# Moving the second half of y behind the third chunk, and the four output products one chunk later, in a Mamba block on one core

## The chip, the cores and the metric

The kernel runs on one core of one Trainium2 chip. The metric is device time in microseconds (us) of one execution, as the median of several runs; less is better. The core has a matrix engine (PE, TensorE; its weight loads are listed apart as PEld), three engines for elementwise work (DVE, VectorE; ACT, ScalarE; POOL, GpSimd), and SP (SyncE), which here only issues transfers. Each engine works through its own queue in order; semaphores tie them together. Matmul results go to PSUM, which has eight banks of 128 x 512 f32.

## The reference, cut to what matters

```python
x = x + attn(cond(x, cond_128, ...), ...)        # the part that this change touches
x = x + ffn(cond2(x, cond_128, ...), ...)

def attn(hidden_states, in_proj_w, conv_weight, ..., norm_weight, out_proj_w):
    proj = einsum('bld,pd->blp', hidden_states, in_proj_w)     # gate z, x, B, C, dt
    xBC = silu(conv(proj[x, B, C]))                            # 4 taps along L
    ...
    def step(state, inp):                                      # 64 heads, 32 steps
        state = state * dA_t + dtx_t * B_t
        return state, einsum('bhpn,bhn->bhp', state, C_t)
    y = ys + x * D
    yn = y * rsqrt(mean(y * y, over a group of 512) + EPS) * norm_weight * silu(gate)
    return einsum('bli,di->bld', yn, out_proj_w)
```

There are 64 sequences of 32 steps with 512 features, 8 groups g of 8 heads each, and 4096 inner features (512 to a group). All data are f32.

## The kernel before

**Tiles and loops.** The 64 sequences are cut into NT = 4 token blocks T of 16 sequences (512 tokens). The main loop (line 939) runs over NI = 32 iterations i, with T, g = divmod(i, 8): one iteration computes one group of heads for one token block. The scan over time is done in closed form: per group, a Gram matrix of B and C, weighted by decays, is multiplied by x. To keep f32 accuracy, the large products run as three f32r products of high and low parts (`mm_split`, line 196: hi by hi, lo by hi, hi by lo). One large product is therefore 12 matmuls of 128 x 512.

**An iteration.** `chunk(i, c)` for c = 0 to 9 (line 429) is one such product of the input projection each: B, C, x0, z0, x1, z1, x2, z2, x3, z3. `evict` (line 460) brings it out of PSUM: a z chunk by one ACT instruction; the B, C and x chunks by one on ACT, three convolution taps on DVE (line 475) and a silu on ACT (line 483). `flip(i, k)` (line 485) transposes x chunk k on DVE into the tile `xs`. `gram(i)` (line 546) makes the Gram matrix in `g_ps` (32 small matmuls), `scan(i)` (line 523) the decays in the tile `src`, on POOL and DVE; `gram_rows` and `decay` (lines 564 and 576) multiply the two.

**y.** `y_part(i, 0, 8)` and `y_part(i, 8, 16)` (line 592) are the two halves of the product of `xs` and `src`: 128 small matmuls of 32 x 32 each (with 128 weight loads), into four banks. The loop over f in it means that the first four matmuls need the x chunks 0 and 1 and the next four the chunks 2 and 3. The first half of iteration i stands at the end of that iteration, the second half in iteration i+1, where it is called with j = i - 1. Then `yend(j, c)`, c = 0 to 3 (line 609), gates a bank of y with z and splits it into `yhi` and `ylo` (a square and a cast on ACT, two instructions on DVE, an addition on POOL); `sumsq(j)` (line 631) reduces the squares.

**Output products.** `out_step(j, bg)`, bg = 0 to 3 (line 909), multiplies `yhi`, `ylo` by the output weights `wo` (`outp`, one large product of 12 matmuls, tile `o`) and adds the result to `acc` on DVE (`outp_end`, line 706, the instruction of line 711). `out_step(j, 1)` first makes the norm's factor: `sumsq2` (line 640), one small matmul `s_ps`, four DVE instructions and a power on POOL. With g = 7 `outp_end` also issues the stores of `acc`, on POOL's queue (on SP's in the last token block).

**Weights of the output product.** `wo_pieces(i)` (line 658) loads `wo` for iteration i in four pieces on SP's queue, one call of `next` a piece. In token block 0 the raw weights are loaded and split by ACT and POOL (`wo_split`, line 679); after that the split weights come from DRAM.

**Order and buffers.** `tc.manual_schedule` (line 922) keeps PE and SP in the order in which the program is written. The other engines' queues are put in order by a planner, from the order of the program and its own estimate of when an instruction can run. Tiles of one tag share a fixed number of buffers: PSUM's tag "mm" has 7 banks, which the chunks, the four banks of a y, the output products and a few others take in turn, the one that was freed first being taken first; `xs`, `src`, `yhi`, `ylo` and `wo` have one buffer each.

PE's order in an iteration from the third on (j > 0) is: chunks 0 and 1, the second half of y(j), chunks 2 and 3, `g_ps`, chunks 4 and 5, o0, chunk 6, `s_ps`, o1, chunk 7, the product of `gram_rows` (`gr_ps`), o2, chunk 8, o3, chunk 9, the first half of y(i). `cond` and `dt_stage` of the next token block, with their own small products, are spread over the iterations with g = 6 and 7, `attend` stands in the one with g = 5.

## Time and profile before

| what | value |
|---|---|
| median of three runs | 1539.41 us (1536.66 to 1543.33) |
| the profiled execution | 1537.98 us, of which the span of all instructions is 1536.2 us |
| PE busy | 98% of the span, mean granted clock 0.993 |
| DVE, ACT, POOL busy | 77%, 41%, 32% |
| DMA engines, mean | 203 GB/s; the instruction queue of PE (q8) 125 packets, 2.05 MB |
| large products of the projection (`mm`, 3840 matmuls) | 926.1 us busy on PE |
| output products (`o`, 1536 matmuls) | 416.0 us busy on PE |
| y (8192 matmuls) | 97.5 us busy on PE |

PE's busy time overstates its work, since matmuls are pipelined: a matmul of 128 x 512 is shown with 390 ns, while two of them start 227 ns apart. A gap of PE is therefore best found in the times at which its loads and matmuls start. The views of waits name for every engine what ended its idle time; "issue" is idle time for which the profile shows no other engine's work as the reason.

### The profile page before, as it was taken

What the parts mean: (1) busy time and instruction counts of PE and PEld (TensorE: products, weight loads), DVE (VectorE), ACT (ScalarE), POOL (GpSimd) and SP (SyncE); (2) the same over time, 40 slices, a digit from 0 to 9 for tenths busy, and PEclk for the clock granted to TensorE, in tenths of its full rate; (3) what the DMA queues carried; (4) which work ended last, traced back from release to release, by engine and by line L of the source; (5) the groups of instructions that cost most, each with busy time, mean ns of one, the idle gap of its engine ahead of it and who ended that gap; (6) DMA issues with size and microseconds to landing.
All of it is one profiled execution on the core that took longest, in us unless ns stands there. A gap on an engine that the chain in (4) does not pass through costs nothing.

```text
span 1536.2 us, 37576 instructions
## 1 busy us (share of the span) xinstructions
PE 1500.2 (98%) x15857; PEld 1226.6 (80%) x15857; DVE 1175.7 (77%) x1869; ACT 637.3 (41%) x1140; POOL 485.4 (32%) x421
## 2 busy tenths in 40 slices
PE   7899999999999999999999999999999999999997
PEld 6788888787788888888878888888888888877776
DVE  7877877888877777779767777887877777777668
ACT  5645555653433333424433332444433323333330
POOL 4656557651522212112331211223242112223105
PEclk9999999999999999999999999999999999999999
DMA  5777777885765555644765555555575555565345
GB/s 205 257 265 272 276 254 260 271 263 186 260 215 198 186 194 193 204 133 150 246 208 191 189 180 179 186 166 178 200 253 186 183 177 166 178 213 173 108 131 172
DMA packets 123305, 311.31 MB, mean 203 GB/s; under 512 B 30528, under 2 KB 42048, under 8 KB 121088
## 3 DMA queue, kind: packets, MB, share of 16 engines
q1 hardware_dynamic: 120320, 301.56, 58.1%
q0 software_dynamic: 2816, 7.34, 1.4%
q8 instruction: 125, 2.05, 0.5%
q14 instruction: 44, 0.36, 0.1%
HBM read 237.02 MB, written 71.83 MB: 201 GB/s over the span
## 4 chain that ended last, share of the span: by engine, by line
PE 86%; DVE 8%; issue 3%; ACT 1%; POOL 1%; DMA 1%; SPq 0%; POOLq 0%; ACTq 0%; DVEq 0%
PE mm L201 53%; PE o L201 21%; PE y L601 6%; DVE x L475 1%; PE fo L201 1%; PE gr_ps L567 1%; DVE ylo L629 1%; PE g_ps L554 1%; PE cv L828 1%; PE h_ps L220 1%; PE d_ps L314 1%; DVE x1s L1211 1%; DVE dt L336 1%; PE lo L871 1%; DVE acc L711 0%
## 5 line engine op out<-in xcount | busy, mean ns | idle before, releaser
L201 PE MATMUL mm<-hid,wsp 128*128 128x512 f32 x3840 | 926.1, 394 | 1.4 <-issue 1.4
L201 PEld LDWEIGHTS mm<-hid,wsp 128*128 128x128 f32 x3840 | 715.5, 189 | 151.3 <-issue 2.1
L625 POOL TENSOR_TENSOR y<-y,y 128x512 f32<-128x512 f32 x96 | 144.4, 1505 | 558.7 <-ACT y L615 554.0
L475 DVE SCALAR_TENSOR_TENSOR x<-mm,xcol,x 128x496 f32<-128x496 f32 (+2 forms) x384 | 271.5, 707 | 36.7 <-ACT x L471 32.3
L201 PE MATMUL o<-wo,yhi 128*128 128x512 f32 x1024 | 278.4, 393 | 0.9 <-ACT wo L682 0.5
L201 PEld LDWEIGHTS o<-wo,yhi 128*128 128x128 f32 x1024 | 189.5, 188 | 40.2 <-ACT wo L682 1.3
L483 ACT ACTIVATE x<-x 128x512 f32<-128x512 f32 x128 | 81.0, 633 | 330.6 <-DVE x L475 329.2
L475 DVE SCALAR_TENSOR_TENSOR B<-mm,pack,B 128x496 f32<-128x496 f32 (+2 forms) x96 | 68.8, 717 | 166.8 <-ACT B L471 164.6
L471 ACT ACTIVATE x<-mm,xcol 128x512 f32<-128x512 f32 x128 | 99.9, 780 | 112.7 <-PE mm L201 111.9
L629 DVE TENSOR_TENSOR ylo<-z,yhi 128x512 fp32r<-128x512 f32 x128 | 142.5, 1114 | 0.5 <-ACT yhi L628 0.4
L201 PE MATMUL o<-wo,ylo 128*128 128x512 f32 x512 | 137.6, 390 | 0.2
L711 DVE SCALAR_TENSOR_TENSOR acc<-o,r,acc 128x512 f32<-128x512 f32 x128 | 95.2, 744 | 32.0 <-POOL r L653 31.9
L601 PEld LDWEIGHTS y<-src,xs 32*64 32x64 f32 x8192 | 89.6, 130 | 33.8 <-issue 26.6
L201 PEld LDWEIGHTS o<-wo,ylo 128*128 128x128 f32 x512 | 96.1, 188 | 21.3 <-DVE ylo L629 1.0
L617 DVE SCALAR_TENSOR_TENSOR z<-y,pack,z 128x512 f32<-128x512 f32 x128 | 94.8, 742 | 20.3 <-ACT y L615 20.2
L653 POOL TENSOR_TENSOR r<-var,mhalf 128x4 f32<-128x4 f32 x32 | 33.8, 1057 | 237.8 <-DVE var L649 237.8
L490 DVE STREAM_TRANSPOSE xs<-x 128x512 f32<-128x512 f32 x128 | 89.8, 702 | 24.4 <-ACT x L483 22.2
L601 PE MATMUL y<-src,xs 32*64 32x32 f32 x8192 | 97.5, 225 | 11.1 <-issue 6.3
L628 ACT CAST yhi<-z 128x512 fp32r<-128x512 f32 x128 | 79.1, 618 | 53.2 <-DVE z L617 53.1
L464 ACT ACTIVATE z<-mm 128x512 f32<-128x512 f32 x128 | 75.8, 593 | 54.7 <-PE mm L201 53.4
L422 POOL TENSOR_TENSOR wsp<-w,wsp 128x512 fp32r<-128x512 f32 x56 | 76.4, 1374 | 57.0 <-ACT wsp L421 56.4
L475 DVE SCALAR_TENSOR_TENSOR C<-mm,pack,C 128x496 f32<-128x496 f32 (+2 forms) x96 | 68.8, 717 | 16.5 <-ACT C L471 14.3
(208 smaller groups left out, 1338.8 us busy)
## 6 DMA issues: line engine op xcount, KB each, us to landing
wsp<-wsp SPq DMA_DIRECT2D x320, 512.0 KB, 4.2
wo<-wos SPq DMA_DIRECT2D x96, 512.0 KB, 4.7
wos<-wo SPq DMA_DIRECT2D x16, 1024.0 KB, 6.2
da<-da SPq DMA_DIRECT2D x124, 128.0 KB, 2.7
w<-in_win_dram SPq DMA_DIRECT2D x48, 256.0 KB, 5.3
wor<-in_wout_dram SPq DMA_DIRECT2D x32, 256.0 KB, 5.1
xr<-in_win_dram SPq DMA_DIRECT2D x24, 256.0 KB, 5.2
acc<-in_x_in_dram SPq DMA_DIRECT2D x4, 1024.0 KB, 6.2
```

The source lines that it names most:

```text
L201: nc.tensor.matmul(o, lhsT=a(k), rhs=b(k), start=j == 0, stop=j == last)
L422: sub_of[n] = nc.gpsimd.tensor_tensor(lo, w, hi.bitcast(F32), ALU.subtract).ins
L471: nc.scalar.activation(t, o, AF.Identity, bias=bias, scale=taps[:, 3:4])
L475: nc.vector.scalar_tensor_tensor(tv[:, :, d:], ov[:, :, : L - d], taps[:, 3 - d : 4 - d], tv[:, :, d:], ALU.mult, ALU.add,)
L483: nc.scalar.activation(t, t, AF.Silu)
L490: nc.vector.transpose(st["xs"][:, :, k], t.rearrange("p (n t) -> p n t", t=L))
L601: nc.tensor.matmul(st["y"][q][64 * f : 64 * f + 64, 32 * n : 32 * n + 32], lhsT=st["xs"][r, n, 2 * f : 2 * f + 2].rearrange("p e x -> p (e ...
L617: nc.vector.scalar_tensor_tensor(z, y, nw_s[:, cc : cc + 1], z, ALU.mult, ALU.mult)
L625: st["add"] = nc.gpsimd.tensor_tensor(y2, st["y2"], y2, ALU.add).ins
L628: nc.scalar.copy(hi, z)
L629: st["lo"] = nc.vector.tensor_tensor(lo, z, hi.bitcast(F32), ALU.subtract).ins
L711: nc.vector.scalar_tensor_tensor(acc[:, bg, :], o, st["r"][:, bg : bg + 1], acc[:, bg, :], ALU.mult, ALU.add)
```

## The change

Two things in the loop are moved; no instruction is added or removed.

The second half of y(j) and the `yend` calls behind it stand after chunk 2 instead of chunk 1 (for j > 0; for j = 0 they stood there before), with `yend` 2 and 3 after chunk 3 and `sumsq` after chunk 4, each one chunk later. The four output products stand after chunks 6, 7, 8 and 9 instead of 5, 6, 7 and 8, so that o3 comes right ahead of the first half of y(i). The start of `wo_pieces(i)`, which needs the buffer that o3 reads, goes from behind chunk 8 to behind chunk 9.

```diff
@@ inner(c)
+            if c == 9:
+                wo_steps = wo_pieces(i)
+                for _ in range(1 if i + 1 < NI else 4):
+                    next(wo_steps)
             if c in (1, 2, 3, 4):
...
-            if c == 8:
-                wo_steps = wo_pieces(i)
-                for _ in range(1 if i + 1 < NI else 4):
-                    next(wo_steps)
@@ the loop
-        if j > 0:
+        chunk(i, 2)
+        inner(2)
+        if j >= 0:
             y_part(j, 8, 16)
             yend(j, 0)
             yend(j, 1)
-        chunk(i, 2)
-        inner(2)
-        if j == 0:
-            y_part(j, 8, 16)
-            yend(j, 0)
-            yend(j, 1)
-        if j > 0:
-            yend(j, 2)
-            yend(j, 3)
...
         chunk(i, 3)
         inner(3)
-        if j == 0:
+        if j >= 0:
             yend(j, 2)
             yend(j, 3)
+        chunk(i, 4)
         if j >= 0:
             sumsq(j)
-        chunk(i, 4)
         inner(4)
...
         chunk(i, 5)
         inner(5)
-        if j >= 0:
-            out_step(j, 0)
...
         if j >= 0:
-            out_step(j, 1)
+            out_step(j, 0)
         next(dt_steps, None)
         chunk(i, 7)
         inner(7)
         if j >= 0:
-            out_step(j, 2)
+            out_step(j, 1)
         step_more()
         chunk(i, 8)
         flip(i, 2)
         if j >= 0:
-            out_step(j, 3)
+            out_step(j, 2)
         inner(8)
...
         chunk(i, 9)
+        if j >= 0:
+            out_step(j, 3)
         inner(9)
         flip(i, 3)
```

PE's order in an iteration is then: chunks 0, 1 and 2, the second half of y(j), chunk 3, `g_ps`, chunks 4, 5 and 6, o0, chunk 7, `gr_ps`, `s_ps`, o1, chunk 8, o2, chunk 9, o3, the first half of y(i).

## The prediction, made before the changed kernel was run

> **What bounds the kernel now.** I read the shares of the engines first, then PE's waits, then the order of time around each of them.

> ```profile
> PE 1500.2 (98%) x15857; PEld 1226.6 (80%) x15857; DVE 1175.7 (77%) x1869; ACT 637.3 (41%) x1140; POOL 485.4 (32%) x421
> ...
> q8 instruction: 125, 2.05, 0.5%
> ```

> ```profile
> PE y L601 <- issue: 6.3, 3, 3.0
> PE y L601 <- DVE xs L490: 4.6, 3, 2.6
> ```

> PE bounds nearly everything, and only its order changes: no matmul is saved, and neighbours of each kind meet as often as before. So the change can only remove or add gaps of PE. I took the start of every load and matmul and, for each product, how much longer it lasted than the median of its kind (2.72 to 2.85 us for 12 large matmuls, 1.42 for half a y). In the stretch that the change reaches, the excess is some 16 us, of three sorts.

> First, the last x chunk turned too late (weight loads at the first halves of y in iterations 5 and 7):

> ```profile
> 279.45 0.21 PEld L601 LDWEIGHTS y<-src,xs 32*64 32x64 f32 x8 [0.35 <-DVE x L475]
> 281.64 1.31 PEld L601 LDWEIGHTS y<-src,xs 32*64 32x64 f32 x120 [1.99 <-DVE xs L490]
> ...
> 374.78 0.21 PEld L601 LDWEIGHTS y<-src,xs 32*64 32x64 f32 x8 [0.35 <-DVE dt L336]
> 377.68 1.31 PEld L601 LDWEIGHTS y<-src,xs 32*64 32x64 f32 x120 [2.69 <-DVE xs L490]
> ```

> Eight loads go, then the ninth waits for `xs`. The excess is 2.12 and 2.83 us, and 0.43 in iteration 1.

> Second, a stop of PE that no engine explains, and what the granted clock does behind it (the windows are the half y and the chunk after it: busy, matmuls, clock, DMA):

> ```profile
> 780.11 1.33 PEld L601 LDWEIGHTS y<-src,xs 32*64 32x64 f32 x123 [0.35 <-issue]
> 784.51 0.20 PEld L601 LDWEIGHTS y<-src,xs 32*64 32x64 f32 x5 [3.07 <-issue]
> ```

> ```profile
> 780.12:784.75 4.63, 1.68 (x130) 1.00 0.92 349
> 784.75:789.19 4.44, 4.44 (x16) 0.62 0.05 17
> ```

> The half y lasts 4.63 instead of 1.42 us, and the next chunk 4.44 instead of 2.81, since the clock fell to 0.62. PE has 32,079 rows in the trace (loads, matmuls, sequencer's own) for the 125 packets of its instruction queue, 257 to a packet of 16,384 bytes. Numbered in order, six stops without a releaser stand before rows 962, 1218, 16321, 22977, 28609 and 30658: all 193 or 194 over a multiple of 256. At each, the row ran 1.27 to 1.48 us after the end of an instruction packet. So PE waited for its next 256 instructions. This falls at y because half a y is 256 instructions in 1.42 us, where a large product is 24 in 2.72.

> Third, o0 had to wait 0.36 us in iteration 7 (`ylo`) and 1.15 in iteration 8 (`wo`, split late on ACT).

> **The change, term by term.** The sum is made for the profiled execution of 1537.98 us (1536.2 span, 1.8 around it), which lies 1.4 below the median; the difference is then taken from the median, 1539.41.

> *Flips.* Between chunk 8 and the first half of y there will be o2, chunk 9 and o3, 8.2 us, instead of o3 and chunk 9, 5.5. That gives nothing by itself where DVE is full. In iterations 5 and 7 it is: from the first `z` to the flip it idled 0.33 and about 1.6 us in 34 and 37. Its queue there:

> ```profile
> 277.25 0.74 DVE L711 SCALAR_TENSOR_TENSOR acc<-o,r,acc 128x512 f32<-128x512 f32 x1
> 277.91 2.21 DVE L475 SCALAR_TENSOR_TENSOR x<-mm,xcol,x 128x496 f32<-128x496 f32 x3
> 280.04 0.74 DVE L711 SCALAR_TENSOR_TENSOR acc<-o,r,acc 128x512 f32<-128x512 f32 x1
> 280.88 0.71 DVE L490 STREAM_TRANSPOSE xs<-x 128x512 f32<-128x512 f32 x1
> ```

> Two things lighten it. The second `acc` is o3's; o3 will end only when y begins, so it falls behind the flip: 0.73. And the three taps of chunk 2 (2.1 us) run while DVE now waits for the second half of y; by the time they end, the old order had 1.25 us of `yend` work done: 0.85 gained. With the 0.1 and some 0.65 of idling, the flips come 1.7 and 2.2 us earlier, so 0.3 and 0.6 of the waits of 2.1 and 2.8 remain. The clock lapse behind the second (the chunk at 379.04 took 4.45, 1.63 too long) goes too, and the 0.43: 0.43 + 1.8 + 2.2 + 1.63 = 6.1 gained. Bounds: 2.1 (only the 0.43 and the clock) to 7.0.

> *o0.* It starts 2.7 us later against `yhi`, `ylo` and the `wo` splits. The splits keep their places in the program; the last `ylo` of an ordinary iteration ended 18.1 us after chunk 0 began, o0 began at 18.7 and will begin at 21.3. Gained 1.5; bounds 0.5 to 1.5.

> *Old instruction stops.* Second halves now begin 24 rows later against the blocks of 256. The stops at 780 (3.2 + 1.63), 1092 (0.39) and 1352 (0.95) lose their alignment: gained 6.2. Those in iteration 1 (its second half isn't moved) and after the loop stay.

> *New instruction stops.* From the rows I placed every boundary. (a) Five iterations (7, 13, 20, 27, 30) get one 11 to 17 rows before the second half, so that the next falls at its end. Before, four lay so (5 to 18 rows ahead): 0, 0, 0.39 and 3.2 us. The 3.2 followed a block that had itself only just landed; the longer way from y to y, 8.4 instead of 5.7 us, prevents that. I take 0.3 each, 1.5; bounds 0 and 4.5. (b) Behind the second half there is now only one chunk ahead of `g_ps`, another 64 rows in 0.39 us:

> ```profile
> 955.64 1.49 PE L601 MATMUL y<-src,xs 32*64 32x32 f32 x128
> 957.05 5.73 PE L201 MATMUL mm<-hid,wsp 128*128 128x512 f32 x24
> 962.72 0.46 PE L554 MATMUL g_ps<-C,B 128*32 128x32 f32 x32
> ```

> Before, a block that began inside the second half had 6.8 us to its end; with one chunk out it has 6.8 - 2.65 = 4.15. Eleven iterations have their boundary 31 to 87 rows into that half. In the same eleven, the packet's start (1.2 to 3.0 us after the block was entered), its length (0.9 to 1.7) and 1.38 us to use gave 3.5 to 5.3 us. Above 4.15 that is 1.14, 0.17, 0.78, 0.48, 0.74, 0.89, 0.19, 0.50, 0.79 and twice nothing: 5.7 lost. Bounds: 0, if the fetch begins earlier, and 11, if DMA is as busy as at the slower half of all fetches.

> [...]

> *At nothing.* PSUM: y's four banks are held one chunk longer, so chunk 3 takes chunk 0's bank; the last tap of B ended 6.1 us after chunk 0's start (638.79 to 644.88), it is needed at 9.8. o3's bank goes to chunk 2, 7 us later; o3's `acc` takes 0.74. If such a cover fails, each microsecond late is one in every iteration. `scan`: `src` is free 2.7 us later, but POOL built it only 7.7 us after y's end (645.87 to 653.61), behind `yend`'s additions, which follow DVE's pace as before. `s_ps`, the norm's factor: shifted with its user. SP: in token blocks 1 to 3 the load of `wo` waits for o3, now 41 us into an iteration, and holds up the load of the next chunk 5, wanted 17 us later (landing 4.2); in block 0 it waits for a raw buffer only. POOL's 20 stores per token block come one chunk later; their readers stand an iteration or more on.

> Sum: -6.1 - 1.5 - 6.2 + 1.5 + 5.7 = -6.6. The profiled execution would take 1531.4, the median 1532.8.

> **Rivals.** (R1) The instruction blocks come in time: 6.6 + 1.5 + 5.7 = 13.8 off, 1525.6. For it: two of eleven were early enough already. Against: the other nine weren't. (R2) DVE stays what the first half of y waits for: where it is full, moving PE's order moves nothing. Then the flips give 0.4 instead of 6.1: 1538.5. For it: 0.33 us of idling in iteration 5. Against: o3's `acc` leaves the queue ahead of the flip. (R3, slower) The planner puts o3's `acc` ahead of the flip, which it precedes in the program, as it did before (280.04 against 280.88). DVE then stands until o3 is done, and y's ninth load waits for 0.44 (o3's end to `acc` at 680.38) + 0.74 + 0.71 less the 0.3 that eight loads and the change of kind take: 1.6 us, in 31 iterations 50: 1583. It decides wherever the planner thinks o3 done when x3's silu is. Against: x3's silu ends some 4 us before o3 does. From five such iterations on, the gain is gone. (R4) The change does less than it says: boundaries drift by a few rows an iteration and new stops match the old: 1540.

> **How the numbers follow.** Forecast 0.5 (own range 1528 to 1538), R1 0.2, R2 0.14, R3 0.1, R4 0.06. With the bounds of the terms and the spread of the runs before (6.7 us), 1523 to 1543 leaves out R3 and a little at both ends. About 0.5% (7.7 us) is what a measurement here can tell from no change, so 1531.7 and 1547.1 divide: the forecast lies just inside "same" and gives a third of its chance to faster (0.17); R1 gives 0.19 to faster; R2, R4 and the rest are same; R3 and a little more slower. Faster 0.37, same 0.51, slower 0.12.

> **What would show it.** Right: no wait of y for `xs` over 1 us; loads of `g_ps` or the end of chunk 3 that start late with "issue", some nine times, under 1.5 us; the stop at 780 gone; o0 never late. Wrong: `acc` (L711) ahead of the flip with PE waiting for `xs` in every iteration; chunk 3 waiting for a tap of B; or "issue" stops over 2.5 us with a clock near 0.6 behind them.

## The result, and the profile after

The changed kernel takes 1544.09 us (median of 20 runs, 1540.14 to 1548.72), the kernel before 1539.38 (20 runs beside them, 1536.21 to 1546.17): ratio 1.0025, 95% interval 1.0015 to 1.0034. That is 4.7 us slower, where 6.6 us less were forecast. The profiled execution took 1543.56 us, its span is 1541.8.

The engines' shares, after:

```profile
PE 1503.3 (98%) x15857; PEld 1227.7 (80%) x15857; DVE 1201.4 (78%) x1869; ACT 633.9 (41%) x1140; POOL 474.4 (31%) x421
```

PE's waits, after (what waited, for whom: us in total, times, longest):

```profile
PE y L601 <- DVE x L475: 4.9, 2, 3.6
PE y L601 <- DVE xs L490: 3.8, 4, 1.1
PE g_ps L554 <- issue: 3.0, 3, 2.5
...
PE y L601 <- issue: 1.4, 1, 1.4
PE o L201 <- DVE ylo L629: 1.0, 1, 1.0
PE o L201 <- ACT yhi L628: 1.0, 1, 1.0
```

The waits of y for `xs` were to fall from 4.6 us to under 1; with those for the taps in front of it (`x`) they are 8.7. The 6.3 us of "issue" at y have become 1.4, and 3.0 stand at `g_ps`. The weight loads of the first half of y in iteration 7, after:

```profile
378.26 0.19 PEld L601 LDWEIGHTS y<-src,xs 32*64 32x64 f32 x4 [0.35 <-issue]
378.85 0.19 PEld L601 LDWEIGHTS y<-src,xs 32*64 32x64 f32 x2 [0.39 <-DVE acc L711]
382.71 0.28 PEld L601 LDWEIGHTS y<-src,xs 32*64 32x64 f32 x2 [3.68 <-issue]
384.26 1.83 PEld L601 LDWEIGHTS y<-src,xs 32*64 32x64 f32 x120 [1.27 <-DVE xs L490]
```

As before, eight loads go and the ninth waits for `xs`, but until 384.26, six microseconds after the first (before: 2.9). The names at the brackets in between are only what ended last by the profile.

**Where the time went.** I compared the length of each iteration, from the end of one first half of y to the end of the next, in three profiles of each kernel (two of each are the last experiment below). Means of three, after less before:

| iterations | us | what stands there |
|---|---|---|
| 0 and 1 | -3.1 | stops of y that differ from one execution to the next |
| 2 | +2.5 | stop at `g_ps` |
| 4 | +0.9 | o0 waits for `ylo`, 1.4 and 0.7 us, in two of the three profiles |
| 5, 6, 7 | +1.3, +1.5, +3.0 | the flip waits and the slow clock behind them |
| 15 and 23 | +0.95 each | flip waits |
| 16, 17, 24, 30 | -1.1, -5.2, -0.6, -0.8 | old stops of PE for instructions |
| the other 19 together | +1.1 | |
| behind the loop | +1.6 | |

The sum is +3.0, the difference of the mean spans (1539.5 and 1542.5); the medians above, of 20 runs each, differ by 4.7. Eleven of the 32 iterations agree within 0.02 us: where nothing stops or is late, the change neither costs nor brings anything.

### The profile page after: what moved, and what is told of

It reads as the page before. It is cut to its first block, busy times and chain, and to the rows that moved or that the text cites. A ratio compares the mean times of both kernels' runs of the same rounds, so it can differ in the third digit from the quotient of the medians.

```text
span 1541.8 us, 37643 instructions
## 1 busy us (share of the span) xinstructions
PE 1503.3 (98%) x15857; PEld 1227.7 (80%) x15857; DVE 1201.4 (78%) x1869; ACT 633.9 (41%) x1140; POOL 474.4 (31%) x421
## 3 DMA queue, kind: packets, MB, share of 16 engines
q8 instruction: 125, 2.05, 0.5%
## 4 chain that ended last, share of the span: by engine, by line
PE 74%; DVE 13%; issue 4%; DMA 3%; POOL 2%; ACT 2%; SPq 1%; POOLq 0%; DVEq 0%; ACTq 0%
PE mm L201 46%; PE o L201 18%; PE y L601 5%; DVE x L475 3%; DVE ylo L629 2%; DMA wor<-in_wout_dram 1%; DMA w<-in_win_dram 1%; DVE src L543 1%; PE fo L201 1%; PE cv L828 1%; DVE z L617 1%; DVE dt L336 1%; PE gr_ps L567 1%; PE h_ps L220 1%; PE g_ps L554 1%
## 5 line engine op out<-in xcount | busy, mean ns | idle before, releaser
L201 PE MATMUL mm<-hid,wsp 128*128 128x512 f32 x3840 | 922.5, 394 | 0.5 <-issue 0.5
L201 PEld LDWEIGHTS mm<-hid,wsp 128*128 128x128 f32 x3840 | 715.2, 189 | 151.2 <-PE cv L828 0.8
L475 DVE SCALAR_TENSOR_TENSOR x<-mm,xcol,x 128x496 f32<-128x496 f32 (+2 forms) x384 | 272.3, 709 | 24.2 <-ACT x L471 17.2
L201 PE MATMUL o<-wo,yhi 128*128 128x512 f32 x1024 | 277.8, 393 | 1.0 <-ACT yhi L628 1.0
L201 PEld LDWEIGHTS o<-wo,yhi 128*128 128x128 f32 x1024 | 189.7, 188 | 39.2 <-ACT yhi L628 1.7
L475 DVE SCALAR_TENSOR_TENSOR B<-mm,pack,B 128x496 f32<-128x496 f32 (+2 forms) x96 | 68.9, 717 | 133.8 <-ACT B L471 131.6
L629 DVE TENSOR_TENSOR ylo<-z,yhi 128x512 fp32r<-128x512 f32 x128 | 160.6, 1273 | 1.3 <-ACT yhi L628 0.3
L711 DVE SCALAR_TENSOR_TENSOR acc<-o,r,acc 128x512 f32<-128x512 f32 x128 | 92.9, 746 | 79.1 <-PE o L201 45.6
L201 PE MATMUL o<-wo,ylo 128*128 128x512 f32 x512 | 137.8, 390 | 1.1 <-DVE ylo L629 1.0
L601 PEld LDWEIGHTS y<-src,xs 32*64 32x64 f32 x8192 | 90.8, 132 | 33.2 <-issue 27.8
L201 PEld LDWEIGHTS o<-wo,ylo 128*128 128x128 f32 x512 | 96.1, 188 | 22.6 <-DVE ylo L629 2.4
L490 DVE STREAM_TRANSPOSE xs<-x 128x512 f32<-128x512 f32 x128 | 90.4, 707 | 26.7 <-ACT x L483 21.1
L601 PE MATMUL y<-src,xs 32*64 32x32 f32 x8192 | 98.8, 227 | 10.5 <-DVE x L475 4.9
L475 DVE SCALAR_TENSOR_TENSOR C<-mm,pack,C 128x496 f32<-128x496 f32 (+2 forms) x96 | 68.9, 717 | 21.2 <-ACT C L471 19.0
L615 ACT ACTIVATE y<-y 128x512 f32<-128x512 f32 x128 | 75.8, 595 | 18.1 <-POOL y L625 13.8
L471 ACT ACTIVATE B<-mm,pack 128x512 f32<-128x512 f32 x32 | 24.9, 779 | 137.9 <-PE mm L201 137.9
```

The costliest lines, as they stand in the source:

```text
L201: nc.tensor.matmul(o, lhsT=a(k), rhs=b(k), start=j == 0, stop=j == last)
L471: nc.scalar.activation(t, o, AF.Identity, bias=bias, scale=taps[:, 3:4])
L475: nc.vector.scalar_tensor_tensor(tv[:, :, d:], ov[:, :, : L - d], taps[:, 3 - d : 4 - d], tv[:, :, d:], ALU.mult, ALU.add,)
L490: nc.vector.transpose(st["xs"][:, :, k], t.rearrange("p (n t) -> p n t", t=L))
L601: nc.tensor.matmul(st["y"][q][64 * f : 64 * f + 64, 32 * n : 32 * n + 32], lhsT=st["xs"][r, n, 2 * f : 2 * f + 2].rearrange("p e x -> p (e ...
L615: nc.scalar.activation(y2, y, AF.Square)
```

## The experiments

All with the kernel before run beside them. "Flip wait" is the excess of the first half of y over 1.42 us; "z's lag" is the time from the end of the second half of y to the first z on DVE, 1.64 us where nothing holds it up.

| label | median us (runs) | ratio to before, 95% |
|---|---|---|
| e1_y_only | 1552.86 (4) | 1.0064, 1.0045 to 1.0084 |
| e2_out_only | 1540.57 (10) | 0.9993, 0.9971 to 1.0015 |
| e3_wo_late | 1537.46 (6) | 0.9968, 0.9953 to 0.9983 |
| e4_gram4 | 1544.59 (10) | 1.0015, 1.0000 to 1.0029 |
| f1_factor_early | 1553.56 (5) | 1.0085, 1.0055 to 1.0115 |
| f2_wo_late_factor | 1543.73 (10) | 1.0026, 1.0007 to 1.0045 |
| f3_acc_behind | 1542.08 (10) | 1.0006, 0.9990 to 1.0023 |
| f4_before_acc | 1533.64 (10) | 0.9956, 0.9937 to 0.9974 |
| g1_before_acc_again | 1534.19 (12) | 0.9962, 0.9944 to 0.9981 |
| g2_wo_late_acc | 1536.87 (12) | 0.9974, 0.9958 to 0.9991 |
| g3_wo_late_again | 1535.61 (12) | 0.9970, 0.9953 to 0.9987 |
| g4_out_wo_late | 1534.37 (12) | 0.9964, 0.9948 to 0.9981 |

### The two halves of the change alone

e1: only the second half of y, `yend` and `sumsq` moved; the output products and `wo` as before. The diffs of this part are against the kernel before.

```diff
-        if j > 0:
-            y_part(j, 8, 16)
-            yend(j, 0)
-            yend(j, 1)
         chunk(i, 2)
         inner(2)
-        if j == 0:
+        if j >= 0:
             y_part(j, 8, 16)
...
```

> Only the second half of y, yend and sumsq are moved; the output products and the start of wo stand as in the kernel before. Theory A (the loss is made in token block 0, where the first raw piece of wo now holds its raw buffer until the later o3 has ended, so that ACT's split waits for its transfer and brings C out late): here o3 ends early again, so the first z instruction comes 1.6 to 2.9 us after the second half of y in iterations 4, 5 and 7 (3.1, 3.5 and 5.2 in the changed kernel). But o0 now follows the last ylo closely, so PE waits 0.2 to 1 us for ylo in most iterations: 10 to 25 us slower than before. Rival B (the later output products are what makes the flips late, through the acc instructions ahead of x3's taps): the flips end relative to y as in the kernel before (+2.1 and +2.9 us in iterations 5 and 7).

Measured 1552.86. o0 waits in nearly every iteration, some 0.5 us (a product of 3.30 instead of 2.8), about 1.5 in four and 3.3 and 3.4 in two. In iteration 2 PE stops for 3.0 us at `g_ps`. PE's wait, e1:

```profile
PE o L201 <- DVE ylo L629: 7.4, 8, 1.2
```

So the output products have to move with y. But z's lag in iterations 4, 5 and 7 is 1.64 to 1.65 here: what makes z late in the changed kernel isn't in this half.

e2: only the output products and the start of `wo_pieces` moved; y as before.

```diff
-            if c == 8:
+            if c == 9:
                 wo_steps = wo_pieces(i)
...
         inner(5)
-        if j >= 0:
-            out_step(j, 0)
...
         inner(6)
         if j >= 0:
-            out_step(j, 1)
+            out_step(j, 0)
...
```

> Only the output products and the start of wo are moved; y stands as in the kernel before. Theory A: ACT still splits wo late in token block 0, so iterations 5 to 7 stay 2 to 5 us longer than before in sum, while the waits for the flips in iterations 15 and 23 (about 1 us each in the changed kernel) are gone, because z starts early again. The stop of 4.8 us at an instruction block in iteration 17 is back, since the second half of y begins at the old row. In all 1540 to 1545 us. Rival B: waits for the flips as in the changed kernel, also in 15 and 23. Rival C (the later y alone makes the loss): iterations 5 to 7 as before or shorter, and the kernel at 1533 to 1538.

Measured 1540.57, no difference from before. z's lag is 2.69, 3.98 and 3.58 us in iterations 4, 5 and 7. In 15 and 23, where y and z stand as they did, the flip ends 1.38 us after the start of y, before 0.20. DVE ahead of that flip in iteration 15, e2:

```profile
722.93 0.51 DVE L649 TENSOR_SCALAR var<-s_ps 32x4 f32<-32x4 f32 x3
723.47 0.43 DVE L336 SCALAR_TENSOR_TENSOR dt<-dt 128x256 f32<-128x256 f32 x1
724.81 1.41 DVE L711 SCALAR_TENSOR_TENSOR acc<-o,r,acc 128x512 f32<-128x512 f32 x2 [0.91 <-POOL r L653]
...
731.30 0.43 DVE L342 SCALAR_TENSOR_TENSOR dt<-dt 128x256 f32<-128x256 f32 x1
731.69 0.71 DVE L490 STREAM_TRANSPOSE xs<-x 128x512 f32<-128x512 f32 x1
```

and before:

```profile
713.27 0.67 DVE L649 TENSOR_SCALAR var<-s_ps 32x4 f32<-32x4 f32 x4 [0.41 <-PE s_ps L644]
714.30 0.29 DVE L329 TENSOR_SCALAR dt<-dt 128x256 f32<-128x256 f32 x1 [0.36 <-ACT dt L327]
715.07 0.75 DVE L711 SCALAR_TENSOR_TENSOR acc<-o,r,acc 128x512 f32<-128x512 f32 x1 [0.48 <-POOL r L653]
```

Before, the norm's factor and the first `acc` were done 14 us ahead of the last flip (729.55); in e2 they come 7 us ahead of it (724.81 to 731.69), two `acc` at once, with a wait of 0.91 for `r`. DVE idles 3.78 us between the first z and the flip (before 2.58) although it has one `acc` less to do.

The stop of iteration 17 was expected back, but it is 0.35 us here, with y where it stood. Stops of 1.55 and 1.23 us stand in iterations 20 and 27 instead (in g4, with the same order of PE, 2.58 and 2.93). PE has 32,084 rows in e2 and 32,079 before: the added rows are waits of its sequencer, and they shift y against the blocks of 256. In iteration 17 the block is entered 18 rows ahead of the second half of y, before 10.

### The raw pieces of wo

e3: the changed kernel; in token block 0 the four raw pieces are loaded behind chunks 1 to 4 of the next iteration instead of behind chunk 9 and chunks 1 to 3, each split one chunk later. g3 is the same kernel, run again beside g1, g2 and g4.

```diff
             if c == 9:
                 wo_steps = wo_pieces(i)
-                for _ in range(1 if i + 1 < NI else 4):
-                    next(wo_steps)
-            if c in (1, 2, 3, 4):
-                if c < 4:
+                if T:
+                    for _ in range(1 if i + 1 < NI else 4):
+                        next(wo_steps)
+            raw = 0 <= j < NG
+            if c in (1, 2, 3, 4, 5)[: 5 if raw else 4]:
+                if c < (5 if raw else 4):
                     wo_split()
                 next(wo_steps, None)
```

> The changed kernel, but in token block 0 the raw pieces of wo are loaded behind chunks 1 to 4 instead of 9 and 1 to 3, so that none waits for o3 in a raw buffer. Theory A: the first z instruction of iterations 4, 5 and 7 comes 1.6 to 2.9 us after the second half of y, iterations 5 to 7 lose 4 to 8 us of their 148.3 in sum, the kernel takes 1536 to 1540. o0 may wait up to 1 us for the last split. Rivals B and C: no change in the waits for the flips, 1543 to 1546.

> e3_wo_late a second time, beside the others on the same chip. If the late raw piece of wo is what the changed kernel lost by (theory A): 1535.5 to 1539, ratio 0.996 to 0.999 again. If the first result (1537.46 of six runs) was chance: 1541 to 1545 like the changed kernel.

Measured 1537.46 and 1535.61: 0.32% and 0.30% below the kernel before that ran beside each, where the changed kernel is 0.25% above it, so some 8.5 us below the changed kernel. The mechanism is seen on ACT at the start of iteration 5. Before (start, length, line, operation):

```profile
241.90 0.62 ACT L682 CAST wo<-wor 128x512 fp32r<-128x512 f32 x1 [0.32 <-DMA wor<-in_wout_dram]
243.01 0.78 ACT L471 ACTIVATE C<-mm,pack 128x512 f32<-128x512 f32 x1 [0.49 <-PE mm L201]
```

The changed kernel:

```profile
242.03 0.62 ACT L682 CAST wo<-wor 128x512 fp32r<-128x512 f32 x1 [3.43 <-DMA wor<-in_wout_dram]
242.56 0.77 ACT L471 ACTIVATE B<-mm,pack 128x512 f32<-128x512 f32 x1
243.23 0.61 ACT L421 CAST wsp<-w 128x512 fp32r<-128x512 f32 x1
245.56 0.62 ACT L682 CAST wo<-wor 128x512 fp32r<-128x512 f32 x1 [1.72 <-DMA wor<-in_wout_dram]
246.08 0.77 ACT L471 ACTIVATE C<-mm,pack 128x512 f32<-128x512 f32 x1
```

With the late pieces (g3):

```profile
237.54 0.62 ACT L682 CAST wo<-wor 128x512 fp32r<-128x512 f32 x1 [1.24 <-DMA wor<-in_wout_dram]
238.07 0.78 ACT L471 ACTIVATE B<-mm,pack 128x512 f32<-128x512 f32 x1
238.75 0.61 ACT L421 CAST wsp<-w 128x512 fp32r<-128x512 f32 x1
239.61 0.78 ACT L471 ACTIVATE C<-mm,pack 128x512 f32<-128x512 f32 x1 [0.25 <-PE mm L201]
```

Chunk 0 began at 237.24, 237.83 and 233.83. So C left PSUM 5.77, 8.25 and 5.78 us behind it; in the changed kernel it stands in ACT's queue behind two casts of `wo` that wait 3.43 and 1.72 us for their loads. Those are late because the first cast, which needs the buffer that o3 reads, can't come before o3 ends: in iterations 5 to 7 it comes 0.7 to 1.5 us ahead of chunk 0, before 4.0 to 6.2 (in iteration 6 o3 had ended 3.5 us earlier, so something else held it there). Until then it keeps one of four raw buffers, and SP's queue, in order, waits for a buffer with all later loads. Behind C follow x0, z and the flips. z's lag goes from 3.52 to 2.17 and 2.07 us in iteration 5, from 5.23 to 3.70 and 3.24 in 7; in 6 and 7 C is still 7.1 to 7.7 us behind chunk 0. Iterations 5 to 7 together last 148.3 us in the changed kernel's first profile, 144.7 and 142.4 in e3 and g3, 141.8 before.

The second part of the gain came as a surprise: the stop at `g_ps` in iteration 2 isn't there either. The weight loads there, after:

```profile
117.61 0.34 PEld L554 LDWEIGHTS g_ps<-C,B 128*32 128x32 f32 x30 [0.35 <-ACT y L615]
120.60 0.14 PEld L554 LDWEIGHTS g_ps<-C,B 128*32 128x32 f32 x2 [2.64 <-issue]
```

and the windows ahead of it, at it, and of the next chunk (busy PE, PEld, DVE, ACT, POOL; then clock, DMA share, GB/s):

```profile
112.60:117.60 5.00, 5.00 (x144) 3.81 (x142) 4.31 (x7) 3.79 (x8) 3.75 (x3) 1.00 1.01 408
117.60:120.78 3.18, 0.65 (x34) 0.48 (x33) 3.18 (x5) 2.61 (x6) 2.94 (x3) 1.00 0.98 352
120.78:125.22 4.44, 4.44 (x16) 3.53 (x13) 4.23 (x8) 2.69 (x7) 4.44 (x3) 0.62 0.80 326
```

The block of instructions was entered at 113.66; the packet of the next began only 4.64 us later, and the row that PE waited for ran 1.38 us after the packet's end. In between the DMA engines were full, with a store of the split `wo` (issued at 112.47), the other split weights and raw loads at once. With the late pieces that store is issued behind the Gram matrix; the same stretch of g3:

```profile
112.60:117.60 5.00, 5.00 (x144) 4.09 (x143) 4.34 (x7) 4.66 (x10) 4.30 (x4) 1.00 0.73 234
```

and the packet begins 0.95 us after the block is entered (1.09 in e3, 1.99 in g2). There is no stop in g3 and e3, and one of 0.42 us in g2.

That the engines were full is not what makes the stop. In h3, a second profile of the changed kernel (below), they were as full at this place (417 GB/s from 117.32 to 121.32), and the packet began 0.92 us after the block was entered, without a stop. What differs is the time of the store of `wo`. In the first profile, h4 and e1 it is issued 1.2 us ahead of the block's entry; the packet begins 4.5 to 4.6 us after the entry, 0.3 to 0.9 us behind the store's landing, and PE stops for 2.6 to 3.0 us. In h3 it is issued 0.65 us ahead. That the packet waits behind the store fits all of these and the late pieces; no run moved the store alone.

### The Gram matrix one chunk later

e4: the changed kernel with `gram` behind chunk 4, away from the second half of y.

```diff
-        late = 2 if i == 0 else 0
+        late = 1 if i else 2
```

> The changed kernel with the Gram matrix behind chunk 4 instead of chunk 3. The instruction block that begins inside the second half of y then has a chunk more to its end (7.1 instead of 4.3 us). If the stops at g_ps come from the instruction fetch, all of them go: iteration 2 loses 4.4 us, iteration 28 0.5, others 0.1 to 0.4: 4 to 6 us below the changed kernel, 1538 to 1540. If they come from something else that g_ps waits for, they stay and the time does too.

Measured 1544.59, as the changed kernel. The stops at `g_ps` in iterations 2 and 28 are gone, 4.40 and 0.55 us less there than in the changed kernel's first profile. That agrees with the reading by instruction blocks, though one profile can't tell it from h3, where the stop is missing too. But the flips are later still: the flip waits are 3.99 and 6.72 us in iterations 5 and 7 (3.49 and 6.48), 1.66 in 15 and 23 (0.96 and 1.13). PE's waits, e4:

```profile
PE y L601 <- DVE xs L490: 6.8, 8, 1.8
PE y L601 <- DVE acc L711: 3.8, 1, 3.8
```

What was won at one place went at the other: z's lag grew to 5.05 and 8.31 us in iterations 5 and 7 (3.52 and 5.23). By which way the later Gram matrix does that was not followed up.

### The norm's factor early, and acc behind the flip

f1: the factor (`sumsq2`, `s_ps`, `r`) right behind o0 instead of behind the product of `gram_rows`, and `acc` of o0 with it.

```diff
     def out_step(i, bg):
-        if bg == 1:
-            sumsq2(i)
-            outp_end(i, 0)
         outp(i, bg)
-        if bg:
-            outp_end(i, bg)
+        if bg == 0:
+            sumsq2(i)
+        outp_end(i, bg)
```

> The changed kernel with s_ps and the norm's factor right behind o0 instead of behind the product of gram_rows, and o0's acc ahead of chunk 7. Theory B (with the output products shifted, the factor comes so late that DVE idles early, and the four var, two acc and the decay stand right ahead of x3's taps): DVE's idling between the first z and the last flip falls from 1.9 us to 1 or less in iterations 15 and 23, the flips end at +0.2 us or earlier against the start of y (1.0 and 1.2 in the changed kernel), iterations 15 and 23 take 45.7 instead of 46.65, iterations 5 and 7 lose about 1 us each: 1539 to 1542 in all. Rival (DVE's work is what fills those iterations, its order doesn't matter): the flips stay, 1543 to 1546.

Measured 1553.56: missed. The flip waits of 15 and 23 grew to 1.66 us each, and one is followed by a slow chunk (1.57). PE's waits, f1:

```profile
PE g_ps L554 <- issue: 5.5, 3, 2.1
...
PE mm L201 <- issue: 3.2, 5, 1.1
...
PE s_ps L644 <- DVE part L637: 2.2, 3, 0.9
```

`s_ps` now waits for the squares (`part`), o0 waits 4.4 us in iteration 8, and the shifted small products put new stops for instructions at `g_ps` and in chunks. The late factor alone therefore doesn't explain the flips of 15 and 23.

f2 is f1 on top of e3; f3 is f2 with `acc` of o2 and o3 held behind the last flip.

> Both repairs: the raw pieces of wo loaded a chunk or more later in token block 0, and the factor right behind o0. If both theories hold, the gains add: 1537.5 less 3 to 5, that is 1532 to 1535, with flips at +0.2 us or earlier in 15 and 23 and below +3 in 5 and 7. If the two repair the same wait, it stays at 1537.

> As the run with both repairs, and o2's and o3's acc behind the last flip. If every instruction ahead of the flip counts, as my sum for o3's acc took it, this brings the flips 0.7 us forward where DVE is full (iterations 5, 7, 15 and 23): 1 to 3 us below the run with both repairs. If o2's bank is then missed, chunk 1 or 2 of the next iteration waits for an acc, and it is slower.

Measured 1543.73 and 1542.08. f2 missed: it shortens iterations 5 to 7 by 7.0 us against the changed kernel, but has stops of 2.86, 1.29 and 1.59 us at `g_ps`. f3 lies 1.7 us below f2, as was expected, but not by the flips: it still waits 1.7 and 1.5 us for those of 15 and 23, and 5.1 in 7 (f2 3.6). The intervals of the two overlap.

f4: the kernel before, with `acc` of o3 alone held behind the last flip; g1 is the same, run again. g2 is e3 with the same hold.

```diff
-        if bg:
+        if bg and not (held and bg == 3):
             outp_end(i, bg)
...
-            out_step(j, 3)
+            out_step(j, 3, True)
...
         flip(i, 3)
+        if j >= 0:
+            with tc.issue_after(state[i]["flip"]):
+                outp_end(j, 3)
+            out_done(j)
```

> The kernel before with o3's acc behind the last flip and nothing else moved: the 0.73 us of my sum by itself. The waits of y for the flip in iterations 5 and 7 (2.1 and 2.8 us) fall by 0.7 each, and the lapse of the clock behind iteration 7 (1.6 us) may go: 1 to 3 us below before. The instruction stops (4.8 us in iteration 17) stay.

> The kernel before with the last output product's accumulation behind the last flip, run a second time. Its first median was 1533.64 us, 6.2 below the kernel before, though its one profile (1537.3, of the slowest of its ten runs) shows the flips no better than before except for 0.15 us each in iterations 15 and 23. If the gain belongs to the kernel: 1531 to 1536 again, ratio below 0.998, and the stop of 4.8 us in iteration 17 missing again in the profile. If it was the luck of the instruction stops in those ten runs: 1538 to 1541, ratio 0.998 to 1.001, and the stop of iteration 17 in place.

> The changed kernel with the raw pieces of wo behind chunks 1 to 4 (as in e3_wo_late) and the last output product's accumulation (0.66 us) behind the last flip, the normalization's factor left where the change has it. If the accumulation ahead of the flip is what makes the flips of iterations 5, 7, 15 and 23 late (+1.62, +4.25, +1.45, +1.16 us in e3_wo_late): 0.3 to 0.7 less in each, 1534.5 to 1537. If the vector engine only waits elsewhere for what it would have done later, as in f3_acc_behind: 1537 to 1540, no difference from e3_wo_late.

f4 and g1: 1533.64 and 1534.19. g2: 1536.87, no difference from g3. The gain of f4 isn't the flips': in g1 they end 2.14 us after y's start in iteration 5 (before 2.14), 2.70 in 7 (2.85), 0.07 in 15 (0.20). DVE in iteration 5, g1 (its lines are two further down):

```profile
278.84 2.21 DVE L475 SCALAR_TENSOR_TENSOR x<-mm,xcol,x 128x496 f32<-128x496 f32 x3
281.80 0.71 DVE L490 STREAM_TRANSPOSE xs<-x 128x512 f32<-128x512 f32 x1 [0.76 <-ACT x L483]
282.44 0.71 DVE L713 SCALAR_TENSOR_TENSOR acc<-o,r,acc 128x512 f32<-128x512 f32 x1
```

From the last tap (281.05) to the flip DVE now idles 0.76 us for the silu on ACT, where before it did the `acc` of 0.74. In iteration 5 the `acc` cost nothing where it was; in 7 and 15 it cost 0.15 and 0.13 us. What f4 and g1 have in common is that iteration 17 lasts 42.69 us instead of 47.50 and iteration 30 0.87 less, 5.7 us together, about the gain in the median. In iteration 17 the packet that PE would wait for begins 0.1 and 0.2 us after the block ahead of it is entered; in three profiles of the kernel before, 3.3 to 3.5. The traces show what goes with that. With the held `acc` PE has 32,100 rows, 21 more waits than before, so the block is entered 19 rows and 2.4 us ahead of the second half of y instead of 10 rows and 1.4 us. A load of `wo` is issued 2.25 to 2.28 us ahead of that half in all five profiles: 0.1 us after the block's entry in f4 and g1, 0.8 to 0.9 us before it in the kernel before. So in these profiles the packet is late where a large transfer was issued shortly ahead of the entry, 0.8 to 0.9 us here and 1.2 at `g_ps` in iteration 2; again no run moved the transfer alone.

### y in its old place, with the late pieces

g4: e2 with the pieces as in e3.

> Only the output products moved, with the raw pieces of wo behind chunks 1 to 4; the second half of y stays behind chunk 2. If the early second half of y gives the vector engine its head start for the flips (the prediction's reading turned round: the move of y behind chunk 3 costs 1.9 us of it, and made the kernel slower by itself in e1_y_only): below e3_wo_late, 1532 to 1536. If the late second half of y pays by the waits of o0 or by where the instruction blocks fall: above it, 1538 to 1542, as e2_out_only at 1540.57 was. The z lag of iterations 5 and 7 should fall from e2_out_only's 3.98 and 3.58 us to 1.7 to 2.9 in either case.

Measured 1534.37. It isn't distinguished from g3 (1535.61; the intervals overlap), so once `wo` is out of the way no gain or loss by the move of y is seen. z's lag is 1.65 us in iteration 5 and 4.62 in 7, the second outside of what was expected, and the flip wait of iteration 5 is nearly gone (its end 0.13 us after y's start; g3 1.53, before 2.14). Its 15 and 23 wait 1.38, as in e2.

### Second and third profiles of both kernels

h1 and h2 are the kernel before, h3 and h4 the changed kernel, as they stand, to see which of the stops belong to a kernel and which to one execution.

> The kernel before, profiled again. If the stop of the second half of y in iteration 17 belongs to it (its instruction block is entered at a place that this order sets): 2.5 to 3.5 us again and a chunk of 4.4 us behind it, the length of the iteration 46 to 48 us. If it is chance: 42.7 us. Flip waits of iterations 5 and 7 2.1 and 2.8 us again, within 0.5.

> The kernel before, a third profile: the same two readings as for h1_before_again.

> The changed kernel, profiled again. If its losses belong to it: flip waits of iterations 5 and 7 of 3 to 4 and 5.5 to 6.5 us, 0.9 to 1.4 in 15 and 23; a stop of 2 to 3 us at the Gram matrix of iteration 2 with a slow chunk behind it, its instruction fetch 4 us or more after the block was entered; no stop in iteration 17. If they were chance: flip waits of 2 to 3 us and an iteration 2 of 42.7.

> The changed kernel, a third profile: the same two readings as for h3_after_again.

Single executions of 1543.75, 1542.21, 1545.72 and 1543.65 us. The stop of iteration 17 belongs to the kernel before; here in h2, the loads and the windows of half y and next chunk:

```profile
784.92 1.33 PEld L601 LDWEIGHTS y<-src,xs 32*64 32x64 f32 x123 [0.36 <-issue]
789.19 0.29 PEld L601 LDWEIGHTS y<-src,xs 32*64 32x64 f32 x5 [2.94 <-issue]
```

```profile
784.92:789.55 4.63, 1.80 (x129) 1.62 (x129) 3.21 (x5) 2.53 (x5) 0.00 (x0) 0.95 0.90 331
789.55:793.79 4.24, 4.24 (x14) 3.40 (x13) 3.62 (x4) 2.10 (x4) 2.89 (x2) 0.65 0.05 15
```

123 loads, then a stop, then five: the same row as in the first profile. In all three profiles of the changed kernel that half y is one run of 128 loads; after:

```profile
780.97 1.38 PEld L601 LDWEIGHTS y<-src,xs 32*64 32x64 f32 x128 [0.35 <-issue]
```

The flip waits belong to the changed kernel too: 3.49, 3.15 and 3.25 us in iteration 5, 6.48, 6.09 and 6.33 in 7, 0.96 to 1.15 in 15 and 23. The stop at `g_ps` in iteration 2 came in two of three (2.77 and 2.64 us); in h3 the packet began 0.92 us after the block was entered, and there was none.

## Why the prediction was wrong

**Flips, predicted -6.1: the step that failed, with three of its parts.** Instead of 6.1 us being gained, iterations 5 to 7, 15 and 23 are 7.7 us longer (means of three). In the first profile of the changed kernel the flip waits there take 12.1 us and the slow clock behind them 3.0; in that of the kernel before both together take 7.0.

1. "The splits keep their places in the program" and, of SP, "in block 0 it waits for a raw buffer only". Both sentences are true of the program and wrong of the time. The first split waits for o3, o3 was moved to the end, and so the raw buffer, SP's queue behind it, the casts and C on ACT's queue came 2 to 3 us late. I followed the load of `wo` in the three later token blocks, and in the first not from the split back to the load. e3 and g3 show what it cost: some 8.5 us. Against the means of the changed kernel, 3.6 and 5.9 us of it are in iterations 5 to 7, 2.1 and 2.7 in iteration 2 (whose stop came in two of three profiles), 1.1 in 4. This one step has more than the distance between the kernels in it, though not all of what was missing to the forecast.
2. "0.85 gained" by the taps of chunk 2. It was a loss. Where nothing else is late the first z came 32.5 us ahead of the first half of y (iteration 10), now 29.8: 2.7 lost, for three taps of 1.9 us that fell out of the stretch. I had read the lag of z in iteration 7 (2.9 us) as the rule; it is 1.64. `ylo` also took longer (last section). In iteration 15 the stretch from z to the flip was to start 2.54 us later and became 1.77 shorter; the flip came 0.77 later.
3. o3's `acc`, 0.73. It did go behind the flip, as forecast, so R3, the rival on the slower side, didn't come. But it had stood under the silu of x3, and its going gave 0.0 in iteration 5 and 0.15 in 7 (g1).

"`s_ps`, the norm's factor: shifted with its user", at nothing, is a fourth one: moved alone, the output products make the flips of 15 and 23 1.2 us later (e2, and g4 again). By which of their instructions is open, as f1 took away the late factor and not the wait.

Two readings in that term were off too. In iteration 5 DVE idled 1.36 us between the first z and the flip (0.8 of it in waits), not 0.33; and 2.1 less 1.7 leaves 0.4 of a wait, not 0.3. Both are small beside what failed.

**o0, predicted -1.5.** The 0.36 of iteration 7 is gone (h1 and h2 had 0.13 at most there). In iteration 8 o0 lost 1.15 to the split of `wo` before; now it loses 1.42, 1.24 and 1.42 in the three profiles, and what it waits for are the last `yhi` and `ylo` (0.35 and 1.43 in the first), which come later with y. In iteration 4 it waits 1.4 and 0.7 for `ylo` in two profiles. So nothing was gained. The working let o0 start 2.7 us later against a last `ylo` that stayed at 18.1 us behind chunk 0. But y was moved as well: in an ordinary iteration (10, 12, 20) the last `ylo` now ends at 20.7 and o0 begins at 21.4, which leaves 0.7 us between them instead of 0.6.

**Old instruction stops, predicted -6.2.** Right. Iterations 17, 24 and 30 are 6.6 us shorter (means of three), 6.0 in the first pair of profiles. Iteration 17's stop belongs to the order, not to chance: three profiles against three. But the shift was not the 24 rows of the working: PE has 23 more waits in the trace (32,102 rows instead of 32,079), and the second halves stand 27 rows later in iteration 2, 40 in 17 and 52 in 31. A fourth stop, of 1.2 and 1.7 us at an output product of iteration 16, stands only in h1 and h2, so the first profile could not give it.

**New stops, (a) +1.5.** None came: by the added rows the five boundaries lie 20 to 40 rows ahead of the second half, not 11 to 17. **(b) +5.7.** The mechanism was right: in iteration 2 the row at `g_ps` ran 1.38 us after the end of its packet. The size was by luck close in the first profile (5.8, of which 4.5 in iteration 2 with the slow clock) and is about 3 in the mean of three. In the first profile six of the eleven places cost nothing and four 0.2 to 0.5, with packets that began 1.3 to 2.4 us after the block was entered where a time is clear. The one dear stop went with a store of `wo` issued 1.2 us ahead of the block's entry, and not with full DMA engines as such: over the 1.5 us after the entry their busy share was 0.89 or more at the other places too. A stop with a clock near 0.6 behind it was among the prediction's own signs of being wrong.

**At nothing, the rest.** PSUM, `scan` and POOL's stores: no wait of a chunk or of `scan` appears. That held.

**The rivals.** R2, DVE stays the bound, was the nearest in mechanism: its flips were to give 0.4. It had no part in which DVE becomes later, which is what happened: by ACT's queue in iterations 5 to 7, and in 15 and 23 without it. R4's first half came true, as the boundaries drifted by about a row an iteration; its second half didn't, as the new stops came to about half of the old. The range (1523 to 1543) left out the result by 1.1 us, as no bound of any term allowed the flips a loss: "2.1 to 7.0". A bound below nothing there was the honest one, for the same text had both the full DVE queue and a second half of y that starts 2.7 us later.

With the cause taken away the forecast isn't reached but its direction is: 1535.6 to 1537.5, 0.3% below the kernel before. The same gain comes without any move of y (g4) or of the products (f4, g1), whose common part is that the stop in iteration 17 is gone. No run shows a gain of the moves beyond that.

**Open.** Why iterations 0 and 1 are 3.1 us shorter and the part behind the loop 1.6 longer; why z still lags 3.2 to 4.6 us in iteration 7 with the late pieces; whether it is the transfer issued ahead of it that makes a packet late, which fits the times given for iterations 2 and 17 but was not tested by itself.

## What to carry to other kernels

When a step is moved, follow every buffer that it frees back to the load that waits for it, and then along each in-order queue that this load or its conversion stands in: here the harm came over a weight buffer, SP's queue and ACT's queue to a chunk that has nothing to do with either. A full engine is hardly relieved by taking an instruction out of a place where it had to wait anyway: here o3's `acc` gave 0.0 us in iteration 5 and 0.15 in 7. Moving instructions can also change the number of waits in an engine's stream (here PE's, by 23), and with it every place at which the stream is cut into blocks (27 to 52 rows at the second halves of y, where 24 were expected). And where stops of several microseconds come and go, take a second profile before counting one of them: iteration lengths agreed to 0.015 us wherever nothing stopped, so three profiles told which stops came every time.

## What the runs showed of the hardware

**A slow clock after short waits.** In g4 the ninth load of y waited 1.23 us in iteration 23, and the next chunk ran at a granted clock of 0.62 (4.44 us instead of 2.81):

```profile
1081.78 1.31 PEld L601 LDWEIGHTS y<-src,xs 32*64 32x64 f32 x120 [1.23 <-DVE xs L490]
```

```profile
1083.14:1087.58 4.44, 4.44 (x18) 3.50 (x14) 0.14 (x2) 0.06 (x1) 0.00 (x0) 0.62 0.44 156
```

**DVE beside POOL.** `ylo` subtracts two tiles. Its mean rose from 1114 to 1273 ns, as it now meets POOL's building of `src`: 30 of 128 begin while that instruction runs and take 1.84 us on average, before 1 of 128 (alone 0.67). In e1, with y moved alone, it is 31, in e2 1. In iteration 15, DVE and then POOL, after:

```profile
711.27 2.46 DVE L629 TENSOR_TENSOR ylo<-z,yhi 128x512 fp32r<-128x512 f32 x2
```

```profile
710.60 1.99 POOL L529 TENSOR_TENSOR src<-dtt,pack 128x1024 f32<-128x1024 f32 x1
```

The first of the two took 1.86 us, the second, begun when POOL was done, 0.68. 1.86 is what was left of POOL's instruction (1.3) and some 0.5 more, a little under the 0.68 that it takes alone.
